# Score products of an attention block in another order: all 128-column products before all 256-column ones

## The chip, the cores and the metric

The kernel runs on one core of a Trainium2 chip. A core has five engines that run side by side and wait for each other through semaphores: TensorE (PE; its weight loads are listed apart as PEld), VectorE (DVE), ScalarE (ACT), GpSimd (POOL) and SyncE (SP), which issues most of the DMA transfers. The results of TensorE go to PSUM, eight banks of 512 floats in each of 128 partitions; this kernel addresses all of them as one tile `banks`. The metric is the time of one launch in microseconds.

## What is computed

One cross-attention layer with 16 heads of 16 columns over 128 sequences of 128 tokens and 256 columns, and a feed-forward part, all in float32:

```python
q = (query @ Wq + bq).reshape(b, s, 16, 16).transpose(0, 2, 1, 3)
k = (key @ Wk + bk) ...;  v = (values @ Wv + bv) ...
scores = jnp.einsum('bhqd,bhkd->bhqk', q, k) / jnp.sqrt(jnp.float32(16))
scores = jnp.where(j < i + mask, scores, NEG_INF)        # mask == 0: keys before the query only
attn = jax.nn.softmax(scores, axis=-1).at[:, :, 0, :].set(0.0)
ctx = jnp.einsum('bhqk,bhkd->bhqd', attn, v)
x = layer_norm(query + ctx @ Wo + bo, ln1_g, ln1_b)
out = layer_norm(x + jax.nn.relu(x @ W1 + b1) @ W2 + b2, ln2_g, ln2_b)
```

Since a query sees only earlier keys, the first 64 queries ("low", `hi` = 0) need only the first 64 keys.

## The kernel before

The 128 sequences are taken in 64 pairs. A step `p` works on several pairs at once, in different stages: the scores and the softmax of pair p, the keys and queries of p+1, the weighing of the values, the output projection and the first norm of p-2, the feed-forward part of earlier pairs. The order of every engine's instructions is written out by hand: `step(p)` walks the list ORDER (L1756 to L1765) and calls what each name stands for; a name with "-1" is that of the pair before. Each call adds its instructions at the end of its engine's queue, so the list gives the order on each engine, and each engine takes its own instructions in that order. Steps 9 to 60 run this list; steps 4 to 8 and 61 to 63 have the same stages with an order of their own, written out call by call.

The names that matter here, in the list's order:

- `weigh` (L576): TensorE multiplies the softmax weights of pair p-2 with its values; the result goes to bank 7 (`at=7`).
- `context` (L606, its instruction L614): VectorE reads bank 7 in two instructions, scales it and writes `cxT`.
- `scores` is `scores_both(p)` (L422, its product L440): 32 products on TensorE. The array is used as eight tiles of 32 rows and 64 columns: a row strip r (0 to 3) for a quarter of the heads, and a column half s for one of the pair's two sequences. In the loop, `strips` is (0, 1) or (2, 3), `m` one of two groups of heads, and `hi` tells low from high queries. A low product streams 128 columns (two heads of 64 keys), a high one 256. Each product is issued as two passes, each with a weight load of its own. High scores of strip r go to bank r, low scores of strip r to bank 4 + r:

```python
st["sps", hi] = [at_bank(r if hi else 4 + r, f"pss{hi}_{p}_{r}") for r in range(NS)]
```

- `maskA0`, `maskA1` (L464) and `maskB` (L456): VectorE adds the mask to the low scores of strip 0, of strip 1, and of strips 2 and 3 at once, reading banks 4, 5, and 6 with 7.
- `add3`, `add1`, `add2`, `add0` (L1562): VectorE adds the mask to the high scores in bank 3, 1, 2, 0; `max3` and so on (L1568) take the maxima.
- `eh7` and so on (L937): ScalarE takes the exponentials of high scores, two heads at a time.
- `v1`, `o1`, `q1` (L1153): the first products on TensorE behind the scores. v1 writes bank 4 and needs maskA0 to be done, o1 bank 5 and maskA1, q1 bank 7 and maskB. `k1`, later in the step, writes bank 3.

In ORDER before, TensorE runs weigh, scores, v1, o1, q1 in this order; VectorE runs context, maskA0, add3, maskA1, maskB, max3.

Of the kernel before, what the change touches and what calls it, by code (L numbers as in the profile page):

```python
# [19 lines left out]
def tile_cross_attention_block(  # L20
# [83 lines left out]
    def weight(w, name):  # L104
        n = w.shape[0] // P
        t = const.tile([P, n, w.shape[1]], F32, tag=name, name=name)
        nc.sync.dma_start(t, w.rearrange("(k p) n -> p k n", p=P))
        return t
# [24 lines left out]
    wk = const.tile([P, KC, D], F32, tag="wk", name="wk")  # L133
# [29 lines left out]
    w1 = weight(W1, "w1")  # L163
# [3 lines left out]
    w2 = weight(W2, "w2")  # L167
# [18 lines left out]
    one = const.tile([1, P], F32, tag="one", name="one")  # L186
# [61 lines left out]
    def at_bank(i, name):  # L248
        return banks[:, i]
# [141 lines left out]
    def room(p, hi):  # L391

        st = states[p]
        if "sm" not in st:
            st["sm"] = wide(f"sm_{p}") if p != 1 else turned_all
        at = H * P if not hi else 0
        n = P if hi else HP
        st["sm", hi] = st["sm"][:, at : at + H * n].rearrange("p (h j) -> p h j", j=n)
        st["nmx", hi] = small.tile([P, H], F32, tag=f"nmx{hi}", name=f"nmx{hi}_{p}")
# [22 lines left out]
    def scores_both(p):  # L422

        st = states[p]
        st["both"] = True
        for hi in range(2):
            st["sps", hi] = [
                at_bank(r if hi else 4 + r, f"pss{hi}_{p}_{r}") for r in range(NS)
            ]
            room(p, hi)  # L430
        one, two = (0, 1), (2, 3)
        for strips, hi, m in (
            (one, 0, 0), (two, 1, 0), (one, 0, 1), (two, 1, 1),
            (one, 1, 0), (one, 1, 1), (two, 0, 0), (two, 0, 1),
        ):
            n = P if hi else HP
            for s in range(2):
                for r in strips:
                    strip, first = slice(32 * r, 32 * r + 32), s * P
                    nc.tensor.matmul(  # L440
                        st["sps", hi][r][
                            s * HP : (s + 1) * HP, m * 2 * n : (m + 1) * 2 * n
                        ].rearrange("p (e j) -> p e j", e=2),
                        st["qT"][strip, m, first + hi * HP : first + hi * HP + HP],
                        st["kT"][strip, m, :, first : first + n],
                        start=True, stop=True,
                    )
# [1200 lines left out]
    def bring_part(p, n):  # L1648
# [3 lines left out]
    OPS = {  # L1652
        "weigh": lambda p: weigh(p - 2),
        "scores": lambda p: scores_both(p),
        "context": lambda p: context(p - 2, True),
        "deviations": lambda p: scales_of(p),
# [96 lines left out]
    for n in range(3):  # L1753
        OPS[f"turn{n}"] = lambda p, n=n: turn(p, n < 2, n % 2)

    ORDER = """  # L1756
        weigh addbo re0-2 vr-1 hf-2 re2-2 re1-2 turnx-1 xc2-1 re3-2 context scores res0 ro3-2
        ro0-2 br1 maskA0 ro2-2 add3 oc0 ro1-2 v1 maskA1 oc2 maskB hs0-1 o1 max3 vk1 vk0 q1
        lowmax eh7 oc1 v2 br0 xs2-1 qk w1-1 hs1-1 ok eh6 tokc-1 w2-1 tokx vk2 el3 oc3 hs3-1 v3
        add1 el4 w5-1 max1 br3 el0 add2 o2 cc0 wk-1 eh3 k1 finish1-1 vb ok2 va eh2 q2 stats2 o3  # L1760
        cc2 kk w6-1 max2 cc1 el6 add0 hs2-1 br2 h1-1 vf el2 ob oa max0 w3-1 qk2 cc3 eh5 xs0-1
        q3 eh0 xs1-1 o4 wk2-1 k2 qa finish2-1 qb hk-1 w7-1 or stats1 kk2 eh4 k3 xc0 means h6-1
        load-1 store-1 eh1 wb-1 xs3-1 ka xc1 wa-1 el5 q4 kb h5-1 xc3 turn1 el1 deviations
        w4-1 hk2-1 turn0 el7 k4 h7-1 res1 hk5-1 turn2 kr h2-1 vs-1 ks ha-1 qr h3-1 ks2 loadx norm2
        hb-1 h4-1 recip norm1 wr-1 turni v4  # L1765
    """.split()

    EMPTY = {'w1': 5, 'h1': 4, 'w2': 5, 'h2': 4, 'w3': 5, 'h3': 5, 'w4': 4, 'h4': 5, 'w5': 4, 'h5': 5, 'w6': 4, 'h6': 5, 'w7': 5, 'h7': 4, 'v1': 3, 'o1': 1, 'q1': 2, 'k1': 2, 'v2': 3, 'o2': 2, 'q2': 2, 'k2': 3, 'v3': 2, 'o3': 2, 'q3': 3, 'k3': 2, 'v4': 2, 'o4': 2, 'q4': 3, 'k4': 2}
# [269 lines left out]
    tokens(5, "c")  # L2038
    bring(3, nc.sync, LATE_FIRST[7:])
    scores_both(4)  # L2040
    mask(4, 0, A)
    mask(4, 1, A)
# [31 lines left out]
    spread_values(4)  # L2074
    stack_values(4)
    scores_both(5)
    tokens(6, "c")
    mask_high(5, 2, 2)
# [1024 lines left out]
```

## Time and profile before

| what | value |
|---|---|
| three runs | 1463.9, 1464.37, 1467.12 us (median 1464.37) |
| the profiled execution | 1463.95 us |
| its span, first to last instruction | 1462.1 us |
| granted TensorE clock, mean | 1.000 |
| score products, L440 | 3840 passes in 60 blocks of 64 |
| HBM over the span | 50 GB/s |

The span is that of the instructions; the time of a launch has 1.85 us more around it. In the timeline a row is a start, a length and a group of like instructions. The ends of matmul passes are modelled, so the drawn length of a block reaches a little into what follows it; starts are exact to some nanoseconds. Idle time of an engine that is not the last one costs nothing.

### The profile page before, as it was taken

What the parts mean: (1) busy time and instruction counts of PE and PEld (TensorE: products, weight loads), DVE (VectorE), ACT (ScalarE), POOL (GpSimd) and SP (SyncE); (2) the same over time, 40 slices, a digit from 0 to 9 for tenths busy, and PEclk for the clock granted to TensorE, in tenths of its full rate; (3) what the DMA queues carried; (4) which work ended last, traced back from release to release, by engine and by line L of the source; (5) the groups of instructions that cost most, each with busy time, mean ns of one, the idle gap of its engine ahead of it and who ended that gap; (6) DMA issues with size and microseconds to landing.
All of it is one profiled execution on the core that took longest, in us unless ns stands there. A gap on an engine that the chain in (4) does not pass through costs nothing.

```text
span 1462.1 us, 62019 instructions
## 1 busy us (share of the span) xinstructions
PE 1445.1 (99%) x20713; PEld 1389.5 (95%) x20713; DVE 1372.1 (94%) x3175; ACT 1302.0 (89%) x5559; POOL 1268.4 (87%) x1872
## 2 busy tenths in 40 slices
PE   9999899999999999999999999999999999999998
PEld 7788799999999999999999999999999999999998
DVE  6987999999999999999999999999999999999777
ACT  5659899999999999999999999999999999999763
POOL 5977898988988988988988988988988988988875
PEclk9999999999999999999999999999999999999999
DMA  8264766766766766766766766766766766765451
GB/s 206 70 143 105 178 158 150 161 160 154 161 160 152 162 158 155 161 159 154 161 155 158 161 155 158 162 162 149 164 154 157 164 152 157 166 158 127 117 131 51
DMA packets 367881, 220.34 MB, mean 151 GB/s; under 512 B 280032, under 2 KB 335584, under 8 KB 367584
## 3 DMA queue, kind: packets, MB, share of 16 engines
q1 hardware_dynamic: 365296, 214.27, 64.2%
q8 instruction: 187, 3.06, 1.0%
q10 hardware_dynamic: 2288, 2.11, 0.7%
q14 instruction: 110, 0.90, 0.2%
HBM read 55.06 MB, written 18.09 MB: 50 GB/s over the span
## 4 chain that ended last, share of the span: by engine, by line
PE 92%; DVE 3%; POOL 1%; ACT 1%; DMA 1%; issue 1%; SPq 0%; POOLq 0%; DVEq 0%; ACTq 0%
PE banks L1153 48%; PE banks L1364 24%; PE banks L440 6%; PE banks L596 4%; PE banks L586 2%; PE banks L875 1%; PE banks L1050 1%; PE banks L300 1%; PE banks L977 1%; ACT sm L937 1%; PE banks L635 1%; POOL sm L476 1%; DVE sm L464 1%; PE banks L1412 0%; PE banks L894 0%
## 5 line engine op out<-in xcount | busy, mean ns | idle before, releaser
L937 ACT ACTIVATE sm<-banks,nmx 128x128 f32<-128x128 f32 x944 | 338.9, 391 | 19.1 <-DVE nmx L1568 15.5
L937 ACT ACTIVATE sm<-sm,nmx 128x64 f32<-128x64 f32 x944 | 323.4, 378 | 0.3 <-DVE nmx L926 0.3
L533 DVE STREAM_TRANSPOSE turned<-sm 128x1024 f32<-128x1024 f32 x186 | 217.1, 1215 | 4.8 <-DMA brought<-turned 3.0
L937 ACT ACTIVATION_READ_ACCUMULATOR sm<-banks,nmx 128x1 f32 x944 | 218.9, 232 | 0.0
L937 ACT ACTIVATION_READ_ACCUMULATOR sm<-sm,nmx 128x1 f32 x944 | 216.4, 229 | 0.0
L1153 PE MATMUL banks<-wt,hS 128*128 128x128 f32 x1344 | 177.7, 275 | 0.0
L1364 PE MATMUL banks<-xS,w1t 128*128 128x128 f32 x1344 | 177.4, 275 | 0.0
L1153 PEld LDWEIGHTS banks<-wt,hS 128*128 128x128 f32 x1344 | 163.6, 192 | 0.1
L1364 PEld LDWEIGHTS banks<-xS,w1t 128*128 128x128 f32 x1344 | 163.5, 192 | 0.1
L1568 DVE TENSOR_REDUCE nmx<-banks 128x4 f32<-128x512 f32 x224 | 152.6, 681 | 1.9
L1557 POOL TENSOR_TENSOR hS<-hT 128x512 f32<-128x512 f32 x116 | 147.8, 1275 | 3.1 <-ACT hT L882 1.4
L1364 PE MATMUL banks<-brought,w 128*128 128x128 f32 x896 | 118.3, 275 | 0.0
L1153 PE MATMUL banks<-w,hT 128*128 128x128 f32 x896 | 109.7, 275 | 0.0
L1364 PEld LDWEIGHTS banks<-brought,w 128*128 128x128 f32 x896 | 109.0, 192 | 0.0
L1618 POOL TENSOR_TENSOR x1b<-x,g_r 128x512 f32<-128x512 f32 x56 | 72.4, 1292 | 39.6 <-ACT x L709 39.6
L1153 PEld LDWEIGHTS banks<-w,hT 128*128 128x128 f32 x896 | 104.8, 192 | 0.0
L440 PE MATMUL banks<-kT,qT 32*64 32x128 f32 (+1 forms) x3840 | 98.4, 331 | 1.8 <-ACT vz L1278 1.5
L1393 ACT ACTIVATE hT<-hT,b1e_c 128x256 f32<-128x256 f32 x224 | 95.6, 509 | 0.3 <-DVE hT L1389 0.2
L1562 DVE TENSOR_TENSOR banks<-banks,neg 128x256 f32<-128x256 f32 x224 | 93.4, 417 | 0.1
L440 PEld LDWEIGHTS banks<-kT,qT 32*64 32x64 f32 x3840 | 79.5, 131 | 12.6 <-ACT vz L1278 1.8
L1219 ACT ACTIVATE kr<-banks,b_c 128x128 f32<-128x128 f32 x224 | 81.8, 403 | 2.7 <-PE banks L1153 2.7
L764 POOL TENSOR_TENSOR t<-t,g_r 128x512 f32<-128x512 f32 x62 | 79.1, 1276 | 5.3 <-ACT t L746 3.9
(324 smaller groups left out, 4795.9 us busy)
## 6 DMA issues: line engine op xcount, KB each, us to landing
brought<-turned SPq DMA_DIRECT2D x936, 128.0 KB, 2.4
out_dram<-t SPq DMA_DIRECT2D x63, 256.0 KB, 4.0
xb<-in_x_dram SPq DMA_DIRECT2D x124, 128.0 KB, 3.3
cb<-in_ctx_dram SPq DMA_DIRECT2D x124, 128.0 KB, 3.3
x<-in_x_dram SPq DMA_DIRECT2D x56, 256.0 KB, 2.9
kT<-kr SPq DMA_DIRECT2D x112, 128.0 KB, 2.2
brought<-turned SPq DMA_DIRECT2D x40, 96.0 KB, 2.5
w<-in_L_xattn_W_dram SPq DMA_DIRECT2D x2, 1024.0 KB, 7.4
```

The lines of the kernel that those rows point to most:

```text
L440: nc.tensor.matmul(st["sps", hi][r][s * HP : (s + 1) * HP, m * 2 * n : (m + 1) * 2 * n].rearrange("p (e j) -> p e j", e=2), st["qT"][strip ...
L533: nc.vector.transpose(turned[:, :, at : at + 256].rearrange("p j (n a) -> p n j a", a=32), states[p]["sm", hi].rearrange("p h j -> p (h j) ...
L764: nc.gpsimd.tensor_tensor(t2, t2, g2_r[:, None, :].to_broadcast([P, 2, D]), ALU.mult)
L937: nc.scalar.activation(sm[:, h, :], src, AF.Exp, bias=nmx[:, h : h + 1], scale=1.0, **({"accum_out": st["su"][:, at : at + 1]} if summed e ...
L1153: nc.tensor.matmul(out, left(k) if self.depth > 1 else left, right(k) if self.depth > 1 else right, start=(n == 1 and k == 0), stop=(k == ...
L1219: nc.scalar.activation(self.k[:, m, s * P : (s + 1) * P], src, AF.Identity, bias=bk_c[:, m : m + 1], scale=1.0,)
L1364: nc.tensor.matmul(ps[:, i * P : (i + 1) * P].rearrange("p (n a) -> p n a", a=32), left(i), right, start=(n in (1, 2, 5) and i == 0), stop ...
L1393: nc.scalar.activation(self.hT[:, f, at], self.hT[:, f, at] if src is None else src, AF.Relu, bias=b1e_c[:, f : f + 1], scale=1.0,)
L1557: engine.tensor_tensor(c[:, n], left, right, how)
L1562: nc.vector.tensor_tensor(ps[:, :, HP:], ps[:, :, HP:], neg[:, 1, None, :].to_broadcast([P, 4, HP]), ALU.add)
L1568: nc.vector.tensor_reduce(states[p]["nmx", 1][:, 4 * b : 4 * b + 4], banks[:, b].rearrange("p (n j) -> p n j", j=P), AX.X, ALU.max, negate ...
L1618: nc.gpsimd.tensor_tensor(st["x1b"], st["x1b"] if n else st["x1"], (be1b_r if n else g1_r)[:, None, :].to_broadcast([P, 2, D]), ALU.add if ...
```

## The change

Two things are reordered. In `scores_both`, every tile's products of 128 columns (hi = 0) come first, in the order strips (0, 1), strips (2, 3), for m = 0 and then m = 1, and those of 256 columns (hi = 1) after them. In ORDER, `maskA1` and `add3` change places. The rest of the list is wrapped anew, with the same names in the same order. `scores_both` is used by all steps from 4 to 63, ORDER by steps 9 to 60.

```diff
         one, two = (0, 1), (2, 3)
         for strips, hi, m in (
-            (one, 0, 0), (two, 1, 0), (one, 0, 1), (two, 1, 1),
-            (one, 1, 0), (one, 1, 1), (two, 0, 0), (two, 0, 1),
+            (one, 0, 0), (two, 0, 0), (one, 0, 1), (two, 0, 1),
+            (one, 1, 0), (two, 1, 0), (one, 1, 1), (two, 1, 1),
         ):
...
-        weigh addbo re0-2 vr-1 hf-2 re2-2 re1-2 turnx-1 xc2-1 re3-2 context scores res0 ro3-2
-        ro0-2 br1 maskA0 ro2-2 add3 oc0 ro1-2 v1 maskA1 oc2 maskB hs0-1 o1 max3 vk1 vk0 q1
+        weigh addbo re0-2 vr-1 hf-2 re2-2 re1-2 turnx-1 xc2-1 re3-2 context scores res0
+        ro3-2 ro0-2 br1 maskA0 ro2-2 maskA1 oc0 ro1-2 v1 add3 oc2 maskB hs0-1 o1 max3 vk1
```

More of the change, by code (lines that the diff above doesn't have):

```diff
@@ L1756, in tile_cross_attention_block @@
     ORDER = """
-        weigh addbo re0-2 vr-1 hf-2 re2-2 re1-2 turnx-1 xc2-1 re3-2 context scores res0 ro3-2
-        ro0-2 br1 maskA0 ro2-2 add3 oc0 ro1-2 v1 maskA1 oc2 maskB hs0-1 o1 max3 vk1 vk0 q1
[L1759 to L1765, printed above, removed]
+        weigh addbo re0-2 vr-1 hf-2 re2-2 re1-2 turnx-1 xc2-1 re3-2 context scores res0
+        ro3-2 ro0-2 br1 maskA0 ro2-2 maskA1 oc0 ro1-2 v1 add3 oc2 maskB hs0-1 o1 max3 vk1
+        vk0 q1 lowmax eh7 oc1 v2 br0 xs2-1 qk w1-1 hs1-1 ok eh6 tokc-1 w2-1 tokx vk2 el3 oc3
+        hs3-1 v3 add1 el4 w5-1 max1 br3 el0 add2 o2 cc0 wk-1 eh3 k1 finish1-1 vb ok2 va eh2
+        q2 stats2 o3 cc2 kk w6-1 max2 cc1 el6 add0 hs2-1 br2 h1-1 vf el2 ob oa max0 w3-1 qk2
+        cc3 eh5 xs0-1 q3 eh0 xs1-1 o4 wk2-1 k2 qa finish2-1 qb hk-1 w7-1 or stats1 kk2 eh4
+        k3 xc0 means h6-1 load-1 store-1 eh1 wb-1 xs3-1 ka xc1 wa-1 el5 q4 kb h5-1 xc3 turn1
+        el1 deviations w4-1 hk2-1 turn0 el7 k4 h7-1 res1 hk5-1 turn2 kr h2-1 vs-1 ks ha-1 qr
+        h3-1 ks2 loadx norm2 hb-1 h4-1 recip norm1 wr-1 turni v4
     """.split()
```

## The prediction

> **What bounds the kernel now.** I read the page from the top, then the chain of waits inside one step, then the timeline of TensorE and VectorE around the score products.
>
> ```profile
> span 1462.1 us, 62019 instructions
> PE 1445.1 (99%) x20713; PEld 1389.5 (95%) x20713; DVE 1372.1 (94%) x3175; ACT 1302.0 (89%) x5559; POOL 1268.4 (87%) x1872
> PE 92%; DVE 3%; POOL 1%; ACT 1%; DMA 1%; issue 1%; SPq 0%; POOLq 0%; DVEq 0%; ACTq 0%
> ```
>
> TensorE is busy 99% of the span and carries 92% of the chain that ended last. VectorE is close behind, so both have to be followed. The chain of waits between 712.15 and 734.2 us holds one whole step, and every piece of it is TensorE (the columns are start, length, what):
>
> ```profile
> 712.19 1.54 PE banks L440 x45
> 713.73 8.23 PE banks L1153 x72
> ...
> 728.89 3.57 PE banks L1364 x32
> ...
> 734.16 0.25 PE banks L440
> ```
>
> From one score block (L440) to the next is 734.16 - 712.19 = 21.97 us, and 1.54 us of it are the block. Whatever the block loses is added to the span, since TensorE has no idle time in the step in which it could catch up. A full-array pass of 128 columns takes 3.57 / 32 = 0.112 us.
>
> Next, the block itself, in the timeline of TensorE, and VectorE over the same time:
>
> ```profile
> 712.12 1.61 PE L440 MATMUL banks<-kT,qT 32*64 32x128 f32 x64
> 713.66 0.71 PE L1153 MATMUL banks<-wv,cT 128*128 128x128 f32 x4
> ...
> 715.10 0.61 PE L1153 MATMUL banks<-xT,wq 128*128 128x128 f32 x4
> ```
>
> ```profile
> 712.26 0.76 DVE L614 TENSOR_TENSOR cxT<-banks,brought 128x256 f32<-128x256 f32 x2
> 713.00 0.42 DVE L464 TENSOR_TENSOR sm<-banks,neg 128x256 f32<-128x256 f32 x1
> 713.34 0.42 DVE L1562 TENSOR_TENSOR banks<-banks,neg 128x256 f32<-128x256 f32 x1
> 713.67 0.41 DVE L464 TENSOR_TENSOR sm<-banks,neg 128x256 f32<-128x256 f32 x1
> 714.00 0.68 DVE L456 TENSOR_TENSOR sm<-banks,neg 128x512 f32<-128x512 f32 x1
> 714.60 0.68 DVE L1568 TENSOR_REDUCE nmx<-banks 128x4 f32<-128x512 f32 x1
> ```
>
> The block is 64 passes (32 products of two) on eight array tiles. The first VectorE row is `context` (L614). It reads what `weigh` left in bank 7, and bank 7 is also where the low scores of strip 3, (two, 0, m), go. So those products cannot start before `context` ends, at 712.26 + 0.76 = 713.02. Does the trace show that wait? Two other steps, in which `context` ran at another time:
>
> ```profile
> 184.61 1.84 PE L440 MATMUL banks<-kT,qT 32*64 32x128 f32 x64
> ...
> 185.02 0.71 DVE L614 TENSOR_TENSOR cxT<-banks,brought 128x256 f32<-128x256 f32 x2
> ```
>
> ```profile
> 1349.56 1.68 PE L440 MATMUL banks<-kT,qT 32*64 32x128 f32 x64
> ...
> 1349.81 0.72 DVE L614 TENSOR_TENSOR cxT<-banks,brought 128x256 f32<-128x256 f32 x2
> ```
>
> From the end of `context` to the end of the block it is 713.73 - 713.02 = 0.71 us, 186.45 - 185.73 = 0.72 and 1351.24 - 1350.53 = 0.71. A `context` that ends 0.23 us later in its block (184.61) makes the block 0.23 longer. The end of the block hangs on the read of bank 7 already. And the one step whose `context` ended before its block began:
>
> ```profile
> 160.47 0.72 DVE L614 TENSOR_TENSOR cxT<-banks,brought 128x256 f32<-128x256 f32 x2
> ...
> 161.28 1.60 PE L440 MATMUL banks<-kT,qT 32*64 32x128 f32 x64 [1.14 <-ACT vz L1278]
> ```
>
> It is 1.60 us long, against 1.61 with the wait. So the order of before hides the read almost wholly: strips 2 and 3 are given their 256-column products first, and the low ones, in banks 6 and 7, come last.
>
> **The change, part by part.** *The order of the products.* (two, 0, 0) moves from seventh place to second. No product, byte or wait is added or removed; the wait for bank 7 moves forward, ahead of nearly everything. Behind it on TensorE then stand all score products but the first group and one tile of the second, and v1, o1 and q1.
>
> What stands behind that wait on the tiles of strip 3 is a chain: each tile runs its eight passes one after another. Before, four passes of 128 columns were left when bank 7 came free, its four of 256 being done. After, all eight are left, for none of strip 3 has run. The addition is four passes of 256 columns per step. Their price:
>
> ```profile
> 83.85 1.51 PE banks L875 x7
> ```
>
> ```profile
> L875 PE MATMUL banks<-brought,w x128: 379/379/483, 78.3 to 1405.8; 128*128 128x256 f32 x128
> ```
>
> By the chain of waits a pass of 256 columns takes 1.51 / 7 = 0.216 us, so 4 x 0.216 = 0.864 us.
>
> Check by the whole chain: the passes end 0.71 us after `context` now. With four more of 0.216 in it they would end 1.57 us after it, so v1 starts about 714.53 where it now starts at 713.66 (0.07 us ahead of the block's drawn end in either case). What is late next is nothing else on TensorE: the tiles of strips 0 and 1 also wait from their third pass on, but they have six passes left where strip 3 has eight.
>
> The refill of weights after the wait isn't shown for so long a row of waiting loads. Bounds: nothing, and one weight load per step, 0.13 us, if a load comes too late for its tile once:
>
> ```profile
> L440 PEld LDWEIGHTS banks<-kT,qT x3840: 127/131/133, 85.3 to 1387.2; 32*64 32x64 f32 x192
> ```
>
> In the other direction, groups of equal length could close up by at most 0.05 us (worked out in the third rival below), but the chain of strip 3 leaves no room for it while the wait stands. I take +0.02, nearer to nothing, since most loads of the block are issued well ahead. That makes 0.88 us per step, between 0.86 and 0.99.
>
> How many steps? `context` has 112 instructions, so 56 uses:
>
> ```profile
> L614 DVE TENSOR_TENSOR cxT<-banks,brought x112: 384/416/426, 138.1 to 1350.1; 128x256 f32<-128x256 f32 x112
> ```
>
> Two are in steps 7 and 8, where it ends ahead of the block or about when bank 6 comes free; 54 (steps 9 to 62) stand as above. Of the six other blocks (3840 / 64 = 60 in all), steps 4, 6, 7 and 63 also write bank 6 or 7 right after another reader. Each loses between nothing and 0.88 us, 0 to 3.5 in all, and I take 2.0: in this part of the kernel TensorE is not always the last.
>
> *maskA1 ahead of add3.* Two VectorE instructions change places, 0.41 against 0.42 us, so nothing is added. Today o1 (bank 5) needs maskA1, which ends at 714.08, and starts at about 714.43, so this gives room that nobody needs. But the order of products makes add3's bank (3, high) the last to be finished. After, maskA0 waits too, because the second group of strips 0 and 1 is queued behind the wait for bank 7: it starts about 0.5 us after 713.02. maskA1 follows, then add3 stands until the whole block ends (some 1.57 us after 713.02, 714.6). maskB goes 0.33 later, and max3 0.6 after that at 715.55. Measured from v1 (714.53) max3 then starts at +1.02, now at 714.60 - 713.66 = +0.94. VectorE comes out about 0.1 us later against TensorE. That is hidden: q1 (bank 7, needs maskB) starts 1.44 us after v1, while maskB would end 1.1 us after it, and later in the step VectorE stands 0.49 us waiting for TensorE:
>
> ```profile
> 723.79 0.29 DVE L1299 TENSOR_TENSOR t<-banks,x1b 128x128 f32<-128x128 f32 x1 [0.49 <-PE banks L1153]
> ```
>
> If that cover were gone, up to 0.1 us per step would come on top, 5.4 us in all. VectorE's added idle time, about 0.5 + 0.4 us, fits into the 0.88 us by which the step grows.
>
> **A rule against the trace.** Does one waiting load hold up the other tiles? Three windows of the block (columns: TensorE busy and passes in flight, weight port busy and loads in flight):
>
> ```profile
> 713.02:713.04 0.02, 0.02 (x12) 0.00 (x0) 1.00 0.00 0
> 713.04:713.07 0.03, 0.03 (x11) 0.03 (x3) 1.00 0.00 0
> 713.07:713.09 0.02, 0.02 (x15) 0.02 (x7) 1.00 0.00 0
> ```
>
> Right after bank 7 is freed the loads in flight go from none to seven, those of strip 2 among them, whose bank 6 was free before: the loads behind the waiting one had waited with it. The Trainium skill, "TensorEngine Tiling (Array Packing)", section Tiling Modes, says that tiles operate independently and load and multiply in parallel. By that rule alone strips 0 and 1 would run on through the wait and the masks would not slip; the sum would stay at 0.86, since strip 3 still has all its eight passes ahead, and the first rival would lose its ground.
>
> **The sum.** 54 x 0.88 = 47.5, and 2.0 for the other blocks: 49.5 us. The profiled execution took 1463.95 us (span 1462.1 and 1.85 around it), 0.42 under the median of the three runs, 1464.37. 1463.95 + 49.5 = 1513.5 us, or 3.4% more.
>
> **The rivals.** *Slower still: VectorE's delay comes back to TensorE.* It decides once maskB ends over 0.3 us later, measured from v1, than now. Against it stand the 0.49 us above and the margin of q1. For it: VectorE is at 94%. Price: 0.1 us per step at least, up to one addition's 0.33. That is 1519 to 1531 us. Chance 8%.
>
> *Slower by less: bank 7 is given up after the first of the two instructions of `context`*, 0.34 us earlier. Then 0.88 - 0.34 = 0.54 us per step, 29 us and the 2: 1495. Against it: the three blocks above all end 0.71 to 0.72 us after the second one. Chance 4%.
>
> *Not slower: the wait for bank 7 doesn't bind in its new place*, because the products of strip 3 need not wait there for `context` (other columns, or the read done by then). It decides where bank 7 is free at most 0.03 us after the block begins. Then every group of eight tiles has one length. A tile needs 0.05 for its first weights, 4 x 0.108 for 128 columns and 4 x 0.216 for 256, which is 1.35, some 0.05 for the last of eight tiles to start, and 0.09 until the full array goes on: 1.49 us, against 1.54 now. 54 x 0.05 = 2.7 us gained, 1461.3, within 0.2%. By the rule of independent tiles this would be the purpose of equal lengths. Against it: the low scores of strip 3 cover columns that `context` reads, and its end moves with the block's in every step looked at. Chance 4%.
>
> **How the numbers follow.** The forecast, 1513.5, has 84%. The range takes the bounds: from 54 x 0.864 = 46.7 with nothing for the other blocks and a little closing up, 1507, to 54 x 0.90 + 3.5 and the uncovered 5.4, about 1522. I set 1505 to 1523. It leaves out the third rival, the second, and part of the first, some 12%. A measurement of this kernel can tell about 0.2% (3 us) from no change. Slower by more: 96%; within it 3% and faster 1%, both from the last rival.
>
> **What would show it.** Right: the block (L440) is drawn 2.45 to 2.5 us long where it was 1.61; its end is about 1.57 us after `context` (was 0.71); no score load starts for about 0.85 us in it; the step is 22.85 us; max3 starts about 1.0 us after v1; the clock stays at 1.00. The VectorE part is wrong if TensorE idles anywhere between v1 and k1. The whole is wrong if the block is 1.5 to 1.6 us long: then the wait of bank 7 was not what ended it, and the last rival holds.

## The result and the profile after

The changed kernel takes 1518.55 us (median of 4 runs, 1517.99 to 1518.62), against 1465.26 us for the kernel before, run beside it: a ratio of 1.0359 (95% interval 1.0343 to 1.0376). It is slower by 53 us. The profiled execution took 1518.62 us, its span is 1516.8 us, 54.7 more than before.

The head of the page after, and two of its costliest groups (columns: busy time, mean ns of one, idle time of the engine ahead of them and what ended it):

```profile
span 1516.8 us, 62013 instructions
PE 1469.4 (97%) x20713; PEld 1388.5 (92%) x20713; DVE 1377.3 (91%) x3175; ACT 1299.4 (86%) x5559; POOL 1272.6 (84%) x1872
...
L440 PE MATMUL banks<-kT,qT 32*64 32x256 f32 (+1 forms) x3840 | 120.0, 332 | 30.1 <-DVE cxT L614 26.9
L464 DVE TENSOR_TENSOR sm<-banks,neg 128x256 f32<-128x256 f32 (+1 forms) x148 | 60.1, 446 | 42.1 <-PE banks L440 38.7
```

TensorE has the same instructions and is busy 97% instead of 99%. The score products (L440) now have 30.1 us of idle time ahead of them, 26.9 of it ended by `context` (L614). The masks of the low scores (L464) wait 38.7 us for score products. The share of the chain that ended last can't be read off the page this time: the view loses the chain after 6% of the span.

One block in the timeline of TensorE, then of VectorE (columns: start, length, what, idle time ahead of it):

```profile
717.00 0.46 PE L440 MATMUL banks<-kT,qT 32*64 32x128 f32 x10
717.95 1.55 PE L440 MATMUL banks<-kT,qT 32*64 32x128 f32 x54 [0.49 <-DVE cxT L614]
719.42 0.71 PE L1153 MATMUL banks<-wv,cT 128*128 128x128 f32 x4
```

```profile
717.14 0.76 DVE L614 TENSOR_TENSOR cxT<-banks,brought 128x256 f32<-128x256 f32 x2
718.57 0.76 DVE L464 TENSOR_TENSOR sm<-banks,neg 128x256 f32<-128x256 f32 x2 [0.67 <-PE banks L440]
719.53 0.43 DVE L1562 TENSOR_TENSOR banks<-banks,neg 128x256 f32<-128x256 f32 x1 [0.21 <-PE banks L440]
719.87 0.68 DVE L456 TENSOR_TENSOR sm<-banks,neg 128x512 f32<-128x512 f32 x1
720.47 0.68 DVE L1568 TENSOR_REDUCE nmx<-banks 128x4 f32<-128x512 f32 x1
```

Ten passes run: the eight of (one, 0, 0) and the two of the first tile of (two, 0, 0). The eleventh is the first that writes bank 7. It starts at 717.95, 0.05 us after `context` ends (717.90), and 53 others follow it. From the first score product to v1 it is 719.42 - 717.00 = 2.42 us, where it was 1.54.

Where the span's 54.7 us came from, by the starts of the score blocks (read from the timelines of both kernels):

| stretch | before, us | after, us | difference |
|---|---|---|---|
| start to block of step 4 | 85.29 | 86.43 | +1.14 |
| block 4 to block 9 | 99.32 | 104.57 | +5.25 |
| block 9 to block 62 (53 steps) | 1164.95 | 1212.00 | +47.05 |
| block 62 to block 63 | 36.28 | 37.95 | +1.67 |
| block 63 to the end | 76.26 | 75.85 | -0.41 |

The 53 steps take 47.05 / 53 = 0.888 us more each. The first row lies ahead of every instruction that was changed; it is spread from run to run (the kernel before ranged from 1463.01 to 1468.00 us over all its runs here). In the profiled execution of the changed kernel TensorE's clock fell to half for 3.4 us at 19 us, in that of the kernel before it did not; all the traces with a fall there need 86.4 to 87.2 us to block 4, those without one 84.2 to 86.0.

### The profile page after: what moved, and what is told of

Read it like the earlier page. It is cut to its first block, busy times and chain, and to the rows that moved or that the text cites. A ratio compares the mean times of both kernels' runs of the same rounds, so it can differ in the third digit from the quotient of the medians.

```text
span 1516.8 us, 62013 instructions
## 1 busy us (share of the span) xinstructions
PE 1469.4 (97%) x20713; PEld 1388.5 (92%) x20713; DVE 1377.3 (91%) x3175; ACT 1299.4 (86%) x5559; POOL 1272.6 (84%) x1872
## 5 line engine op out<-in xcount | busy, mean ns | idle before, releaser
L937 ACT ACTIVATE sm<-banks,nmx 128x128 f32<-128x128 f32 x944 | 343.8, 409 | 28.5 <-DVE nmx L1568 22.4
L937 ACT ACTIVATE sm<-sm,nmx 128x64 f32<-128x64 f32 x944 | 331.2, 402 | 0.2 <-DVE nmx L926 0.2
L937 ACT ACTIVATION_READ_ACCUMULATOR sm<-sm,nmx 128x1 f32 x944 | 239.4, 254 | 0.0
L937 ACT ACTIVATION_READ_ACCUMULATOR sm<-banks,nmx 128x1 f32 x944 | 235.2, 249 | 0.0
L440 PE MATMUL banks<-kT,qT 32*64 32x256 f32 (+1 forms) x3840 | 120.0, 332 | 30.1 <-DVE cxT L614 26.9
L440 PEld LDWEIGHTS banks<-kT,qT 32*64 32x64 f32 x3840 | 76.2, 131 | 53.2 <-DVE cxT L614 39.9
L464 DVE TENSOR_TENSOR sm<-banks,neg 128x256 f32<-128x256 f32 (+1 forms) x148 | 60.1, 446 | 42.1 <-PE banks L440 38.7
L1219 ACT ACTIVATE kr<-banks,b_c 128x128 f32<-128x128 f32 x224 | 89.5, 438 | 3.2 <-PE banks L1153 3.2
```

The source lines that it names most:

```text
L440: nc.tensor.matmul(st["sps", hi][r][s * HP : (s + 1) * HP, m * 2 * n : (m + 1) * 2 * n].rearrange("p (e j) -> p e j", e=2), st["qT"][strip ...
L464: nc.vector.tensor_tensor(st["sm", hi][:, 4 * r : 4 * r + 4, :], st["sps", hi][r][:, : 4 * n].rearrange("p (n j) -> p n j", j=n), no[:, No ...
L937: nc.scalar.activation(sm[:, h, :], src, AF.Exp, bias=nmx[:, h : h + 1], scale=1.0, **({"accum_out": st["su"][:, at : at + 1]} if summed e ...
L1219: nc.scalar.activation(self.k[:, m, s * P : (s + 1) * P], src, AF.Identity, bias=bk_c[:, m : m + 1], scale=1.0,)
```

## The experiments

**The two halves of the change.** Only `maskA1` and `add3` exchanged, with the old order of products (lines cut at the end, "..."):

```diff
-        ro0-2 br1 maskA0 ro2-2 add3 oc0 ro1-2 v1 maskA1 oc2 maskB hs0-1 o1 max3 ...
+        ro0-2 br1 maskA0 ro2-2 maskA1 oc0 ro1-2 v1 add3 oc2 maskB hs0-1 o1 max3 ...
```

> The kernel before with only maskA1 and add3 exchanged on VectorE; the score products keep their old order. Theory (the read of bank 7 is what costs): no change, 1464 to 1467 us, score block 1.61 us long, since o1 is not late today. Rival (the VectorE order has a share in the 53 us): at least some 5 us slower than before.

1464.78 us, ratio 0.9999 (0.9989 to 1.0009): no change. The block is 1.61 us long as before:

```profile
647.08 1.61 PE L440 MATMUL banks<-kT,qT 32*64 32x128 f32 x64
648.62 0.71 PE L1153 MATMUL banks<-wv,cT 128*128 128x128 f32 x4
```

Only the new order of products, with `add3` ahead of `maskA1` as it was:

```diff
-            (one, 0, 0), (two, 1, 0), (one, 0, 1), (two, 1, 1),
-            (one, 1, 0), (one, 1, 1), (two, 0, 0), (two, 0, 1),
+            (one, 0, 0), (two, 0, 0), (one, 0, 1), (two, 0, 1),
+            (one, 1, 0), (two, 1, 0), (one, 1, 1), (two, 1, 1),
```

> The changed kernel with add3 put back ahead of maskA1. Theory: the score block costs the same 0.89 us per step, but add3 now waits for the end of the block ahead of maskA1, so maskA1 and with it o1 come late: about 0.2 us of TensorE waiting per step between v1 and o1 or before q1, 54 x 0.2 = 11 us more than the changed kernel, 1526 to 1532 us. Rival (the exchange on VectorE does nothing): 1518 us.

1535.66 us, ratio 1.048 (1.0465 to 1.0496): 17 us slower than the whole change, more than the 11 expected. The step is 23.17 us against 22.86, so it is 0.31 us per step and not 0.2. VectorE, then TensorE, in one step of it:

```profile
680.82 0.42 DVE L464 TENSOR_TENSOR sm<-banks,neg 128x256 f32<-128x256 f32 x1 [0.67 <-PE banks L440]
681.79 0.43 DVE L1562 TENSOR_TENSOR banks<-banks,neg 128x256 f32<-128x256 f32 x1 [0.54 <-PE banks L440]
682.13 0.41 DVE L464 TENSOR_TENSOR sm<-banks,neg 128x256 f32<-128x256 f32 x1
```

```profile
682.23 0.39 PE L1153 MATMUL banks<-wvt,cc 128*128 128x128 f32 x2
682.69 0.68 PE L1153 MATMUL banks<-wo,cxT 128*128 128x128 f32 x4
```

`add3` (681.79) stands until the block has ended, `maskA1` ends at 682.54 behind it, and o1 starts at 682.69, 0.46 us after the products ahead of it where it is 0.23 in the changed kernel (719.97 and 720.20); o1 itself takes 0.08 longer (0.52 to the next products against 0.44). The two make the 0.31. The exchange is no gain in itself; it is what the new order needs so as not to cost more.

**Is it the bank's wait, or the order itself?** The weighed values go to bank 3 instead of bank 7, in steps 7 to 62, in either kernel:

```diff
-        "weigh": lambda p: weigh(p - 2),
+        "weigh": lambda p: weigh(p - 2, 3),
```

Bank 3 holds high scores of strip 3. In the old order these stand second, in the new one sixth and last. First with the old order:

> The kernel before, its old order of products, with the weighed values written to bank 3 (high scores of strip 3) instead of bank 7, steps 7 to 62. Theory (what counts is how much of a strip's chain stands behind the read of its bank): strip 3's high products stand second, so eight passes follow the read, as in the changed kernel: 949 + 68 + 4 x 216 + 3 x 108 + 198 = 2403 ns from the first score product to v1 instead of 1538, 0.86 us per step, 1465 + 47 = 1512 us (1508 to 1516). Rival (the cost comes from the new order, groups of equal length that change weights all at once): 1465 us.

1519.13 us, ratio 1.0363 (1.0346 to 1.038): the kernel before, with its order untouched, becomes as slow as the changed one. TensorE in one step:

```profile
668.88 0.67 PE L440 MATMUL banks<-kT,qT 32*64 32x128 f32 x10
669.83 1.55 PE L440 MATMUL banks<-kT,qT 32*64 32x256 f32 x54 [0.28 <-DVE cxT L614]
671.31 0.71 PE L1153 MATMUL banks<-wv,cT 128*128 128x128 f32 x4
```

Again ten passes, a stop until `context` has ended, 54 passes. To v1 it is 671.31 - 668.88 = 2.43 us (2.40 expected), and the step is 22.86 us. The total is 7 us over what was expected (3 us over the range). Steps 9 to 62 have 47.6 us of it, as expected. In the profiled execution, which is 3 us shorter than the median, another 3.3 us lie between blocks 4 and 9, most of them in steps 5, 7 and 8 (in 5 and 8 TensorE's clock fell to half for 3.4 us), and 1.5 between blocks 62 and 63.

Then with the new order:

> The changed kernel with the weighed values in bank 3 instead of bank 7, steps 7 to 62. Theory: in the new order strip 3's high products come last, so only four passes of 256 follow the read: 949 + 68 + 3 x 216 + 304 = 1969 ns to v1, 0.43 us per step over before, 23 us, and some 6 us of the other blocks: 1494 us (1490 to 1499). Rival (cost of the new order itself): 1518 us as before.

1502.28 us, ratio 1.0256 (1.0238 to 1.0275): 16 us faster than the changed kernel, by moving one buffer.

```profile
661.85 2.03 PE L440 MATMUL banks<-kT,qT 32*64 32x128 f32 x64
663.82 0.71 PE L1153 MATMUL banks<-wv,cT 128*128 128x128 f32 x4
```

To v1 it is 1.97 us, as expected to the last digit, and the steps up to 40 take 22.40 us, 0.43 over before. The total is 8 us above what was expected, since from about step 40 on the steps grow to 23.6 us; that is taken up below. Two kernels with the same order differ by the bank, and two with different orders agree when the bank is moved so that the same chain stands behind it. The rival, that the order itself makes the cost, falls.

**The wait taken away.** In steps 9 to 62 `context` reads the inverse sums, which lie in SBUF, in place of bank 7. The weighed values are left out, TensorE's work and VectorE's instructions stay:

```diff
             pc = states[p].pop("pc").rearrange(parts, m=KC, s=2, l=2, q=2)
+            if p >= 7:
+                pc = states[p]["inv"]
```

> The kernel before; in steps 9 to 62 VectorE's two instructions after the weighing read the inverse sums from SBUF in place of bank 7, so the weighed values are left out and no score product waits for VectorE's read of bank 7. Theory: the old order hides the wait but for 0.01 us per step (1.60 against 1.61 us): 1464 to 1466 us. Rival (the wait costs the old order too, 0.05 us or more): 1462 us or less.

1468.11 us, ratio 1.0013 (1.0004 to 1.0023). The steps get shorter by 0.014 us (21.956 against 21.970), as small a gain as expected; the total is 2 us over the expected range, of which the stretch from block 62 to 63 has 1.2 (37.50 against 36.28).

> The changed kernel with the same part left out, so that its score products no longer wait for the read of bank 7. Theory (the wait is the whole cost of steps 9 to 62): the score block takes about 1.56 us to v1, as in the changed kernel's step 8, which has no wait (1.26 + 0.30), against 1.54: 54 x 0.025 = 1.4 us and the other blocks' 6: 1472 us (1469 to 1475). By groups of equal length that close up to 1.49 us per block: 1469 us or less, block 0.05 shorter than before. Rival (the order itself costs): 1500 us or more.

1491.44 us, ratio 1.0171 (1.0153 to 1.0188): 27 us under the changed kernel, but not the 1472 expected. Steps 10 to 35 take 22.00 us, 0.04 over the mate above, as the theory has it. Then they grow, to 23.7 at step 60. What TensorE's weight port mostly waited for between 300 and 1350 us (columns: total us, times, longest):

```profile
PEld banks L1155 <- DVE sm L464: 16.2, 42, 0.4
PEld banks L1155 <- issue: 8.4, 18, 1.8
PEld banks L440 <- issue: 4.5, 3, 1.8
```

"issue" is time in which an engine waits for nothing that the profile shows. Neither the kernel before nor the changed one has more than 0.2 us of it there.

**Why the steps grew.** First thought: instructions that had not arrived, so fewer of them should help. Both kernels without the wait, less the 100 empty instructions per step that stand between TensorE's products:

```diff
-    EMPTY = {'w1': 5, 'h1': 4, 'w2': 5, 'h2': 4, ...
+    EMPTY = {}
```

> The changed kernel without the wait for bank 7 (nowait_after), and without the 100 empty instructions per step that follow TensorE's products. Theory (from step 40 on its TensorE stood for instructions that had not been fetched yet): 100 of some 1000 instructions fewer per step, so no idle time of that kind (issue) and steps of about 22.0 us to the end; 1469 to 1476 us. Rival (the lost 20 us come from waiting for another engine or for data): steps still grow to 23 us and more, 1485 us or over.

> The kernel before without the wait for bank 7 (nowait_before), without the empty instructions, as a mate to the run above. Theory: they cost or bring little here, 1464 to 1470 us; the difference between the two is then the order of products alone, 54 x 0.04 us in steps 9 to 62 and about 4.5 us in the other blocks, 5 to 8 us.

1494.16 and 1487.60 us, one run each. The expectation fell: without the empty instructions the old order too loses some 20 us, and both have idle time put to issue (in the second 14.4 us ahead of weight loads of scores). So it isn't their number that hurts. The records of one step's TensorE instructions, counted from block to block:

```
kernel               MATMUL LDWEIGHTS NOP EVENT_SEMAPHORE   sum
before, after           328       328 100              12   768
weigh3_before           328       328 100              12   768
nowait_before           328       328 100              12   768
weigh3_after            328       328 100              13   769
nowait_after            328       328 100              13   769
nowait_after_nopad      328       328   0              13   669
nowait_before_nopad     328       328   0              12   668
```

And from the page's list of DMA queues (packets, MB, share), the same in the kernels before and after but for the share:

```profile
q8 instruction: 187, 3.06, 0.8%
```

TensorE has 47,924 records in the kernel before, and 47,924 / 187 = 256.3: one packet for every 256 instructions, 16 KB. 768 is three packets. With 768 instructions per step the packets' borders stay at one place of the step; with 769 they move by one instruction per step. With 769 the steps grow from about step 36 or 41 on; with 669 and 668 every second or third step is up to 1.8 us longer, from the start; kernels with 768 show neither. The test is to take out one empty instruction per step:

```diff
-    EMPTY = {..., 'v1': 3, ...
+    EMPTY = {..., 'v1': 2, ...
```

> The changed kernel without the wait for bank 7 (nowait_after), with one empty instruction fewer behind v1 in each step: 768 TensorE instructions per step, as before, instead of 769 (without the wait on VectorE a semaphore instruction of its own had come in). Theory (TensorE's instructions come in blocks of 256; 768 is three of them, and one more per step shifts the blocks against the step until a fetch falls into the score block): no idle time put to issue, all steps 22.00 us, 1472 us (1469 to 1475). Rival (the growing steps have another cause, in the products' order or in an engine that falls behind): steps grow after step 40 again, 1485 us or over.

1476.73 us, ratio 1.0071 (1.0054 to 1.0088), 1.7 us above the range; the rival falls. All steps are 22.00 us to the end, and between 300 and 1350 us one group of waits is left at the weight port, none of them issue:

```profile
PEld banks L1155 <- DVE sm L464: 18.5, 48, 0.4
```

One instruction fewer of 769 gives back 15 us.

The traces show the packets at work. Between 260 and 1360 us TensorE's queue stands for more than 0.56 us 11 times in nowait_after, 6 times in weigh3_after, and 15 and 16 times in the two kernels without empty instructions. All 48 stops come at the same place of a packet: the number of TensorE records ahead of the stop, divided by 256, leaves 193 or 194. And each stop ends 1.18 to 1.59 us after a 16 KB packet of queue q8 has landed; in one of the longest of nowait_after the packet lands at 1281.28 and the queue goes on at 1282.73. The kernel before and nowait_after_768 have no such stop. So TensorE stands for its next packet.

With 768 instructions the comparison without the wait is clean (TensorE, new order, then old order):

```profile
655.66 1.63 PE L440 MATMUL banks<-kT,qT 32*64 32x128 f32 x64
657.23 0.71 PE L1155 MATMUL banks<-wv,cT 128*128 128x128 f32 x4
```

```profile
646.34 1.59 PE L440 MATMUL banks<-kT,qT 32*64 32x128 f32 x64
647.86 0.71 PE L1155 MATMUL banks<-wv,cT 128*128 128x128 f32 x4
```

1.57 us to v1 in the new order, 1.52 in the old. Of the 0.888 us per step, 22.858 - 22.00 = 0.86 go with the wait; without the wait the new order costs 0.03 to 0.04, so it gains nothing. While the wait stands this cost isn't seen: weigh3_before, in the old order, has the same step of 22.86 us.

**Steps 4 to 8 and 63.** The new order in steps 9 to 62 alone, and in the others alone (in short: `new` and `old` stand for the two lists, and the second run has `not 9 <= p <= 62`):

```diff
-        for strips, hi, m in (
+        for strips, hi, m in (new if 9 <= p <= 62 else old):
```

> The changed kernel with the old order of products in steps 4 to 8 and 63. Theory: steps 9 to 62 make 54 x 0.888 = 48 us and the rest, some 5 to 6 us, is TensorE waiting in steps 4 to 8 for VectorE instructions whose hand-written order was that of the old products, with a lower clock in step 5: 1513 us (1511 to 1515), clock 1.000 between 110 and 115 us. Rival (all of the 53 us comes from steps 9 to 62): 1518 us.

> The other half: the new order of products in steps 4 to 8 and 63 alone, and maskA1 ahead of add3. Theory: 1465 + 5 to 7 us = 1471 us (1469 to 1473), with the clock down in step 5. Rival: 1465 us, no change.

1513.38 us, ratio 1.0324 (1.0306 to 1.0342), and 1469.84 us, ratio 1.003 (1.002 to 1.0041). The parts add up: 48.0 + 4.4 = 52.4 of the 53 us. Of the 5.25 us between blocks 4 and 9, step 4 has 0.89, step 7 has 1.49 and step 5 has 2.89. Step 5 in the timeline of TensorE, before and after:

```profile
107.92 1.99 PE L300 MATMUL banks<-xT,wq 128*128 128x256 f32 x8 [1.10 <-DVE sm L464]
```

```profile
111.41 2.93 PE L300 MATMUL banks<-xT,wq 128*128 128x256 f32 x6 [2.53 <-DVE sm L464]
```

The query products wait 2.5 us for a mask where they waited 1.1. In step 5's written order VectorE takes the high scores of strips 2 and 3 ahead of that mask, and these are now the last to be finished. Here the pause is followed by a slower clock, in the windows view of the changed kernel (columns: stretch, length, busy time of the engines, then granted clock, DMA share, GB/s):

```profile
109.00:111.00 2.00, 0.00 (x0) 0.00 (x0) 1.90 (x3) 0.00 (x0) 0.00 (x0) 1.00 0.63 150
111.00:113.00 2.00, 1.59 (x4) 1.32 (x5) 1.97 (x5) 1.86 (x11) 0.00 (x0) 0.58 0.66 155
113.00:115.00 2.00, 2.00 (x7) 1.61 (x6) 1.93 (x5) 2.00 (x13) 0.00 (x0) 0.56 0.70 168
```

The half clock is not a mark of the new order, though. In swap_alone, with the old order and its pause of 1.10 us, the same eight products take 3.50 us instead of 1.99, and the clock is down:

```profile
106.81 3.50 PE L300 MATMUL banks<-xT,wq 128*128 128x256 f32 x8 [1.10 <-DVE sm L464]
```

```profile
107.00:109.00 2.00, 2.00 (x6) 1.62 (x6) 1.97 (x4) 2.00 (x14) 0.00 (x0) 0.53 0.67 156
```

In weigh3_after, with the pause of 2.53 us, the clock stayed at 1.00; its step 5 took 20.99 us, where the changed kernel took 22.40 and the kernel before 19.51. So 1.48 of the 2.89 us are the longer pause. The other 1.41 go with the clock and can be absent in another execution; step 6 of weigh3_after was 0.90 longer, so less may be saved in all.

To see whether that mask's place is what counts, `order_edges` with the mask moved:

```diff
+    mask(5, 0, A)
     mask_high(5, 2, 2)
     exponential_by_head(5, 1, range(8, 12), True)
     exponential_by_head(5, 1, range(12, 16), True)
-    mask(5, 0, A)
```

> The kernel with the new order of products in steps 4 to 8 and 63 alone (order_edges), and in step 5 VectorE's masks of the low scores of strips 0 and 1 moved ahead of the mask, maxima and exponentials of the high scores of strips 2 and 3. Theory (in step 5 TensorE stands until VectorE, in its old order, gets past high scores that now come last, and its clock drops behind that pause): the pause of 2.5 us ahead of the query product shrinks to about 1 us, the clock stays at 1.00 between 109 and 115 us, and 2 to 4 us of the 4.5 go: 1466 to 1468 us. Rival (the loss of steps 4 to 8 is again the wait for bank 6 or 7): no change, 1470 us.

1470.91 us, ratio 1.0037 (1.0023 to 1.005): nothing gained, and the time is the one that the rival gave. The pause ahead of the query products is gone and the clock is 1.00 there, as the theory had it, but a pause of the same kind stands ahead of the next key products, and the clock falls behind that one (0.50 between 119 and 121 us):

```profile
117.16 2.91 PE L300 MATMUL banks<-cT,wk 128*128 128x256 f32 x8 [2.05 <-DVE mv L657]
```

So step 5 loses to VectorE's work on high scores that come late, and not at one mask. What an order of VectorE made for the new products would save there wasn't tried.

For steps 4 and 7 the rival holds: the products of strip 3 or 2 wait there for a bank that ScalarE still reads (`hT`). Step 4 of the changed kernel:

```profile
86.43 0.45 PE L440 MATMUL banks<-kT,qT 32*64 32x128 f32 x10
87.43 1.55 PE L440 MATMUL banks<-kT,qT 32*64 32x128 f32 x54 [0.55 <-ACT hT L882]
```

From the first score product to the product behind the block it is 2.48 us, where it was 1.59; in step 7 it is 2.55, where it was 1.65. Both are the 0.88 us of the steady steps again.

## Why the prediction came out right, and where it was off

- *The wait for bank 7 moves ahead of strip 3's chain, 0.88 us per step.* Right: 0.888. The block ends 719.50 - 717.90 = 1.60 us after `context`; 1.57 was forecast. The four passes of 256 make 0.864; the rest, 0.024, was put down to the refill of weights, taken as 0.02, which no run here separates. That the bank and the chain behind it decide is shown by moving the bank in both orders, and by taking the wait away.
- *One waiting load holds all that stands behind it.* Right. No further product runs between the tenth and the eleventh (columns: TensorE busy and passes, weight port busy and loads):

```profile
717.00:717.08 0.08, 0.08 (x5) 0.08 (x10) 1.00 0.00 0
717.08:717.94 0.86, 0.37 (x10) 0.13 (x10) 1.00 0.00 0
717.94:718.10 0.16, 0.15 (x8) 0.16 (x16) 1.00 0.00 0
```

  In the 0.86 us no load is added to the first ten, though strips 0 and 1 needed no bank that VectorE was reading. The rule of the Trainium skill, "TensorEngine Tiling (Array Packing)", section Tiling Modes, that tiles work independently, holds for their streams of passes but not past a load that waits for a semaphore.
- *VectorE's delay of 0.1 us is hidden.* Right: max3 starts 720.47 - 719.42 = 1.05 us after v1 (1.02 forecast), and TensorE doesn't stop behind v1. (maskA0 starts 0.67 us after `context`, not 0.5, which costs nothing.) The rival in which the delay comes back does not occur, but only because `maskA1` was moved: the forecast called that room which nobody needs. That is so in the old order (no change alone); in the new order it saves 0.31 us per step.
- *Groups of equal length would close up to 1.49 us without the wait.* Wrong, without weight for the sum: 1.57 us, 0.05 more than the old order's 1.52. The forecast left out that the passes of all eight tiles then ask for new weights at about the same time; that this is the reason was not tested.
- *The other blocks, 2.0 us, at most 3.5.* Too small: 5.25 in blocks 4 to 8, and 0.4 from the end of block 62 on. The wait for banks 6 and 7, which is all that the forecast priced there, came as taken: 0.89 us in step 4, 0.02 in step 6, 0.90 in step 7 and 0.14 in step 63, 1.95 in all. What it put at nothing is that VectorE's order in these steps was written for the old order of products, so that TensorE's next products wait longer for its masks: 1.43 us more in step 5, 0.56 in step 7. The last 1.4 is the clock in step 5, which the forecast wanted to stay at 1.00; it did so only in steps 9 to 62.
- *The range.* Its upper end was built with 0.90 us per step, though 0.99 had been given as the bound; with 0.99 it would have been 1526 us. Nothing hangs on it here.
- The sum: 54 x 0.888 = 48.0 where 47.5 was forecast, the other blocks 5.6 where 2.0 was, and 1.1 us ahead of the change. No experiment beat the kernel before: the order of before already hides the wait but for 0.014 us per step, 0.8 us in all.

## What to carry to other kernels

Before products are reordered, list for each group the buffer it writes and who still reads it: what a moved wait costs is the longest chain that stands behind it, here eight passes instead of four. Moving the buffer can undo as much as reordering. Where two variants differ by much more than their stages do, count the instructions of each engine per step: one more or less can shift the fetches. And look at the clock in more than one trace before a change is blamed for its fall.

## What the hardware showed that was not expected

TensorE's instructions come in packets of 256, 187 of them here, and a step with 768 instructions stays in phase with them. With 769 per step TensorE began to stand for instructions after some 30 steps, at the end up to 1.7 us per step. With 669, and with 668 in the old order (1487.6 us), the stops came every second or third step. All 48 stops of more than 0.56 us lie at one place of a packet and end 1.2 to 1.6 us after one has landed.

TensorE's granted clock falls to half for 3.4 us, or twice that, in some executions, and the length of the pause ahead of it does not settle whether it does. Behind the pause of 2.5 us in step 5 (new order) it fell in six traces of seven; behind that of 1.1 us (old order) it fell in two of six, and behind the stops of 0.5 us in steps 9 to 62 never. The spread between the runs of one kernel goes with it: beside the experiments the kernel before took 1463.0 to 1463.7 us in its nine runs with a mean clock of 1.000, and 1464.6 to 1468.0 us in the nine with 0.996.
